# Conditional attention on one NeuronCore: the value products moved behind output blocks in a hand-written order

## The chip, the cores and the metric

The kernel runs on one core of a Trainium2 chip. The metric is the device time of one launch in microseconds. Most executions of one kernel agree within 0.3%.

## The reference, cut to what matters

For each of 16 batches (D = 512 channels, T = 1024 tokens, 8 heads of 64) the reference computes attention in which queries, keys and values are one projection, with a 0/1 mask per token, and adds the result to the input:

```python
q = transpose(x) @ Wq.T                       # T x D
scores = scale * einsum('bhqd,bhkd->bhqk', qh, qh)
logits = (scores * cmask + (1.0 - cmask) * NEG) * rmask
attn = softmax(logits)
out = (attn @ qh) @ Wo.T
y = x + transpose(out)
```

About half of the tokens are active. A masked key gets no weight. A masked query has only zeros for logits, so it averages all values.

## The kernel before, in words

The active tokens of a batch (384 to 544 of 1024) are gathered into C = 544 slots: four blocks of 128 and a tail of 32. Everything below runs over slots. Masked rows get the mean's product, added to their rows and written out as well.

For each batch, in this order of need:

- `xt`: TensorE transposes the gathered rows (L424), and ACT and DVE split them into two float16 parts, `xh` and `xl` (L384, L385).
- `query(n, e, g)`: 12 products with the query weights (L447) for channel block e (0 to 3) and column half g, into a `pm` tile in PSUM. ACT copies it out as q (L450), DVE masks it (L453).
- `qsplit`: DVE makes two float16 parts `hl` of q (L461 to L463), and four DMAs on SP's queue spread them by head into `xx` (L468 to L471). These DMAs are handed to `later`, and are issued at the next step.
- `value(n, e)`: eight short products (L497) of `xx` with a constant turn q's block e into tokens by channels, in a `pm` tile. ACT copies it out as v (L500). Its squares are summed by head into `sd` (L480 on ACT for e = 0, L484 on DVE for the others, L485). `value_tail` does this for the 32 tail tokens (L520).
- the shift, that is the largest squared norm of each head, which keeps the exponential in range, in three parts, for one half g of the heads: `peaks` (DVE, L541 and L543, into `smcol`), `top` (a TensorE transpose, L549, and a DVE maximum `m`, L551), `bottom` (a small product that broadcasts `m`, L558, and DVE and ACT steps from L560 on that make `nm`, the exponential's bias, and `corr`).
- `scores(b, p, i)`: four products per head and row block (L620) into a `pss` tile, of which there are two; ACT takes the exponential and its row sums (L624). The tail's scores are L595 and L599.
- `attend`: p times v, summed in `pav` (L643, the tail L647); ACT copies it out as `c` (L651).
- `recip_sums` and `recip_rows`: the reciprocal row sums, transposed (L680, copied by L683) and sent through DRAM (`rd`, `rb`; L685, L688); `norm` multiplies `c` with `rb` (L711 on) and splits it into `ch` and `cl`.
- `project(o, i)`: 12 products with the output's weights (L727) for row block i; DVE adds them to the gathered rows (L732), and POOL scatters these to the output (L811). `project_tail` does it for the tails of three batches at once, in every third batch.

`pm` has two buffers. All products named except scores and attention take a `pm` tile in turn, so each waits until the one two places earlier has been read out.

The order is written by hand in `run`. One loop runs over batches b. While the scores and attention of b run (18 steps), a list `m` of other work is spread between them: the rest of batch b's own preparation (fourth value, second half of the shift), the output of batch o = b - 1, and the x transposes, queries, values and first half of the shift of batch n = b + 1. Each entry is a cost and a function. `fill` calls entries until their summed cost reaches the step's share, so an entry's place in `m` and the costs ahead of it decide between which scores it stands. Costs in use: value 0.45 (`value` of the own batch) or 0.25, query 1.37, projection 2.6, top and bottom 0.1 each, the others mostly 0. A tile scheduler then arranges the instructions of each engine close to the order of these calls; entries under `high_priority` may come earlier. Each engine takes its instructions in order.

The names in `m`: `sums`, `rows`, `second`, `third` are the reciprocal steps of o's last head pair and the norms of its pairs 2 and 3; `x` the five transposes; `pk`, `tp`, `bt` are peaks, top and bottom; `q` query with qsplit; `v` value; `tc`, `tv` the tail's copy and value; `P_` the output block; `tail` the tail's output; `rng` range checks; `hot`, `index`, `take` prepare and gather batch b + 2; `rest` adds the mean to masked rows.

Of the kernel before, what the change touches and what calls it, by code (L numbers as in the profile page):

```python
# [49 lines left out]
class Fast:  # L50
# [794 lines left out]
    def run(self, flag):  # L845
        B = self.B
        L = lambda f, *a: lambda: f(*a)
# [5 lines left out]
        def xt(n):  # L853
            return [(0.45, L(self.xt, n, c)) for c in range(4)] + [(0.25, L(self.xt, n, 4))]

        def query(n, e, g):
            u = [(1.37, L(self.query, n, e, g))]
            return u + [(0, L(self.qsplit, n, e))] if g else u

        def value(n, e):  # L860
            return [(0.45, L(self.value, n, e))]

        def project(o, *i):
            return [(2.6, L(self.project, o, k)) for k in i]
# [80 lines left out]
        if True:  # L945
            for b in range(B + 1):
                o, n = b - 1, b + 1
# [3 lines left out]
                free, sums, rows, third, tail, rest = {}, [], [], [], [], []  # L951
                if b:
                    sums, rows, third = [(0, L(self.recip_sums, o, 3))], [(0.1, L(self.recip_rows, o, 3))], [(0, L(self.norm, o, 3))]
                if n < B:
                    if b in tails:
                        free[0] = [L(self.late, o, 4)]
                        tail = [(2.6, L(self.project_tail, o))]
# [3 lines left out]
                second = [(0, L(self.norm, o, 2))] if b else []  # L961
                P_ = (lambda *i: project(o, *i)) if b else (lambda *i: [])
                pk, tp, bt = ((lambda o, g, f=f, c=c: [(c, L(f, o, g))]) for f, c in ((self.peaks, 0), (self.top, 0.1), (self.bottom, 0.1)))
                new = [g for g in groups if b == g[0] - 2], [g for g in groups if b == g[0] - 1]
                if n < B:
                    q, x, v = (lambda e, g: query(n, e, g)), xt(n)[2 if b == 0 else 0:], (lambda e: [(0.25, L(self.value, n, e))])
                    tc, tv = ((lambda g, f=f, c=c: [(c, L(f, n, g))]) for f, c in ((self.tail_copy, 0), (self.value_tail, 0.25)))
                    rng = [(0, L(self.range_x, n, c)) for c in range(DC)]
                    ahead = b + 2 < B
                    hot, index = ([(c, L(f, b + 2))] if ahead else [] for f, c in ((self.hot, 0), (self.index, 0.2)))  # L970
                    take = [(0, L(self.gather, b + 2, j)) for j in range(5)] if ahead else []
                    m = sums + x[:2] + (value(b, 3) if b else []) + pk(b, 1) + second + x[2:4] + rows + x[4:]
                    for g in new[0]:
                        m += [(0, L(self.active, *g))]
                    m += q(0, 0) + tp(b, 1) + (q(0, 1) if b else bt(b, 1) + q(0, 1))
                    for g in new[0]:
                        m += [(0.3, L(self.slots, *g))]
                    for g in new[1]:
                        m += [(0, L(self.facts_sums, *g))]
                    m += (bt(b, 1) if b else hot) + q(1, 0) + third + ([] if b else index) + q(1, 1) + ([] if b else take)  # L980
                    for g in new[1]:
                        m += [(0.1, L(self.facts_end, *g))]
                    m += rng[:2] + tc(0) + tail + v(0) + P_(0) + tv(0) + rest + v(1) + P_(1) + (hot if b else []) + rng[2:] + q(2, 0) + (index if b else [])
                    m += pk(n, 0) + q(2, 1) + tp(n, 0) + P_(2) + (take if b else []) + q(3, 0) + v(2) + bt(n, 0)
                    m += q(3, 1) + tc(1) + [(0, L(self.means, n))] + P_(3) + tv(1)
                    if b == 0:
                        k = next(k for k, (c, f) in enumerate(m) if f is index[0][1])
                        for c in range(DC):
                            m.insert(k + 1 + 3 * c, (0, L(self.split, "o", c)))
                else:  # L990

                    places = [("xi", 8), ("xa", 13)]
                    come = [[L(self.late, x, j, *places[k % 2]) for j in range(5, 9)] for k, x in enumerate(rests[b])]
                    leave = [[L(self.rest, x, j) for j in range(5, 9)] for x in rests[b]]
                    free[0] = [L(self.late, b, 4)] + come[0]
                    for c, l in zip(come[1:] + [[]], leave):
                        free[0] += c + l
                    m = second + sums + value(b, 3) + pk(b, 1) + rows + [(0.6, lambda: None)]
                    m += tp(b, 1) + [(0.6, lambda: None)] + bt(b, 1) + [(2.6, L(self.project_means, b))] + third + [(1.2, lambda: None)] + P_(0, 1, 2, 3)
# [4 lines left out]
                if b == 0:  # L1004
                    m = begin + m
# [204 lines left out]
```

## Time and profile before

| what | value |
|---|---|
| median of 3 runs | 1081.12 us (1079.87 to 1084.78) |
| the profiled execution | 1081.4 us |
| its span, first to last instruction | 1079.7 us |
| mean granted TensorE clock | 0.995 |
| busy: TensorE matmul, weight load | 1038.1 us, 690.9 us |
| busy: DVE, ACT, POOL | 745.6 us, 681.6 us, 303.0 us |
| DMA moved | 181.39 MB, mean 168 GB/s |

The profile is that of one execution. The busy time of an engine is the time that its instructions cover; matmuls overlap, and a matmul's own duration is longer than its distance to the next. A row such as `PE pm L497 <- DMA xx<-hl: 11.4, 15, 1.9` says that TensorE sat idle ahead of the instruction at line 497, which writes the tile pm, until the DMA from hl into xx had landed: 11.4 us in total, 15 times, 1.9 us the longest. A timeline row gives start and duration in us, engine, line, operation, output and input, shapes, count, and in brackets the idle time ahead of it. A row of windows gives a stretch of the span, its length, the busy time of each engine with the number of its instructions, the granted clock, the mean busy share of the DMA engines and what they moved in GB/s. Operations recorded as L497 are those that this line of the kernel issues.

### The profile page before, as it was taken

Reading aid. Unit: us, or ns where it says so; the run is one execution under the profiler, and the core shown is the slowest. Engines: PE = TensorE matmul, PEld = TensorE weight load, DVE = VectorE, ACT = ScalarE, POOL = GpSimd, SP = SyncE. Lnnn points to the kernel's source line nnn. Section 1 sums busy time; section 2 is a strip of 40 time slices with the busy share of each in tenths; the row PEclk is TensorE's granted clock in tenths of the full one; section 3 lists DMA queues with packets and bytes.
Section 4 is the critical chain, followed back from the end, with each engine's and each line's share of the span. In section 5 each row is a group of like instructions: output and inputs, shape, how many; then the busy total and the mean of one; then the engine's idle time right before and its main releaser. Section 6 shows DMA issues by size and latency. Waiting matters only on the chain.

```text
span 1079.7 us, 23837 instructions
## 1 busy us (share of the span) xinstructions
PE 1038.1 (96%) x8626; PEld 690.9 (64%) x8626; DVE 745.6 (69%) x2376; ACT 681.6 (63%) x1722; POOL 303.0 (28%) x303
## 2 busy tenths in 40 slices
PE   6889999999999999999999999999999999999996
PEld 6566667666666666666666666667666665666553
DVE  6687768676675767766785776868667775666553
ACT  5777667666676766666576666666666565665550
POOL 3101022222202223222233323222232331335652
PEclk9999999999999999999999999999999999999999
DMA  6746465556655554656556566554755554565752
GB/s 205 211 126 177 133 175 154 174 150 190 174 141 158 171 173 145 198 176 169 177 147 197 154 186 193 152 171 135 229 176 173 177 149 127 149 182 166 222 175 84
DMA packets 78125, 181.39 MB, mean 168 GB/s; under 512 B 15008, under 2 KB 16800, under 8 KB 78000
## 3 DMA queue, kind: packets, MB, share of 16 engines
q1 hardware_dynamic: 56816, 111.62, 36.6%
q0 software_dynamic: 21184, 68.18, 20.8%
q8 instruction: 70, 1.15, 0.5%
q14 instruction: 55, 0.45, 0.1%
HBM read 92.34 MB, written 33.91 MB: 117 GB/s over the span
## 4 chain that ended last, share of the span: by engine, by line
PE 82%; DMA 7%; DVE 3%; ACT 2%; issue 2%; SPq 2%; POOL 0%; POOLq 0%; ACTq 0%; DVEq 0%
PE pav L643 21%; PE pss L620 19%; PE pm L727 15%; PE pm L447 14%; DMA xx<-hl 6%; PE pm L424 3%; PE pav L647 3%; PE pss L595 2%; PE pm L497 2%; PE pm L680 1%; ACT q L450 1%; SPq L470 1%; ACT p L624 1%; PE pm L520 1%; DMA rb<-rd 1%
## 5 line engine op out<-in xcount | busy, mean ns | idle before, releaser
L624 ACT ACTIVATE p<-pss,nm 128x544 f32<-128x544 f32 x512 | 365.5, 717 | 210.5 <-PE pss L620 203.6
L620 PE MATMUL pss<-xx 128*128 128x272 f16 x2048 | 317.6, 280 | 3.1 <-ACT p L624 2.7
L643 PE MATMUL pav<-p,v 128*64 128x272 f32 x2048 | 262.9, 399 | 0.0
L620 PEld LDWEIGHTS <-xx 128*128 128x128 f16 x2048 | 191.9, 100 | 73.2 <-issue 27.7
L643 PEld LDWEIGHTS pav<-p,v 128*64 128x64 f32 x2048 | 135.6, 136 | 94.3 <-issue 27.1
L811 POOL DMA_INDIRECT y_out<-xa,idx x68 | 70.2, 1032 | 288.6 <-issue 91.5
L447 PE MATMUL pm<-xh,wqh 128*128 128x274 f16 (+1 forms) x512 | 143.3, 280 | 3.3 <-DVE nm L560 1.9
L447 PE MATMUL pm<-xl,wqh 128*128 128x274 f16 (+1 forms) x512 | 142.9, 279 | 0.2 <-DVE xl L385 0.2
L447 PE MATMUL pm<-xh,wql 128*128 128x274 f16 (+1 forms) x512 | 143.0, 279 | 0.0
L339 POOL DMA_INDIRECT xa<-x_in,idx x68 | 69.5, 1023 | 167.1 <-PE pss L620 71.0
L447 PEld LDWEIGHTS <-wqh 128*128 128x128 f16 x1024 | 99.3, 98 | 25.9 <-issue 6.7
L811 POOL DMA_INDIRECT y_out<-xi,idx x60 | 74.0, 1233 | 137.7 <-DVE xi L798 38.3
L624 ACT ACTIVATION_READ_ACCUMULATOR p<-pss,nm 128x1 f32 x512 | 102.6, 200 | 0.0
L450 ACT ACTIVATE q<-pm 128x272 f32<-128x272 f32 (+1 forms) x128 | 50.8, 397 | 81.6 <-PE pm L447 81.6
L727 PE MATMUL pm<-woh,ch 128*128 128x512 f16 x240 | 91.8, 382 | 0.3 <-DVE tmp L523 0.3
L727 PE MATMUL pm<-wol,ch 128*128 128x512 f16 x240 | 91.7, 382 | 0.0
L727 PE MATMUL pm<-woh,cl 128*128 128x512 f16 x240 | 91.5, 381 | 0.0
L732 DVE SCALAR_TENSOR_TENSOR xa<-pm,xa 128x512 f32<-128x512 f32 x60 | 41.4, 690 | 72.4 <-PE pm L727 72.3
L339 POOL DMA_INDIRECT xi<-x_in,idx x60 | 61.3, 1021 | 106.1 <-PE pss L620 49.5
L727 PEld LDWEIGHTS <-ch 128*128 128x128 f16 x480 | 46.7, 98 | 45.6 <-issue 2.2
L369 ACT ACTIVATE xm<-xm 128x1024 f32<-128x1024 f32 (+1 forms) x62 | 62.5, 1009 | 2.3 <-DMA xm<-x_nat_in 2.3
L711 DVE TENSOR_TENSOR c<-c,rb 128x544 f32<-128x544 f32 x64 | 46.1, 720 | 22.4 <-PE pss L620 11.1
(194 smaller groups left out, 1550.0 us busy)
## 6 DMA issues: line engine op xcount, KB each, us to landing
xx<-hl SPq DMA_DIRECT2D x256, 136.0 KB
xm<-x_nat_in SPq DMA_DIRECT2D x56, 512.0 KB
rb<-rd SPq DMA_DIRECT2D x128, 136.0 KB
pt<-c SPq DMA_DIRECT2D x64, 136.0 KB
pt<-p SPq DMA_DIRECT2D x64, 136.0 KB
ub<-ud SPq DMA_DIRECT2D x16, 256.0 KB
xi<-x_nat_in SPq DMA_DIRECT2D x8, 256.0 KB
xa<-x_in,idx POOLq DMA_INDIRECT x68, 4.5
```

The source lines that it names most:

```text
L339: dma = self.nc.gpsimd.indirect_dma_start(out=tile[:n], out_offset=None, in_=self.x, in_offset=bass.IndirectOffsetOnAxis(ap=idx, axis=0))
L369: self.nc.scalar.activation(s["xm"][k], s["xm"][k], AF.Copy, accum_out=s["ms2"][:, k:k + 1])
L424: self.pe = nc.tensor.transpose(pt[:, c, :], x[:n, c * P:(c + 1) * P], self.ident[:n, :n]).ins
L447: self.beat = nc.tensor.matmul(pq, lhsT=w[:, c, e * P:(e + 1) * P], rhs=xx[:, c, cols], start=(k == 0), stop=(k == 3 * DC - 1)).ins
L450: nc.scalar.activation(s["q"][:, e, cols], pq, AF.Copy, scale=1.0 / (SX * SW))
L620: self.beat = nc.tensor.matmul(pt[:, g, :CH], lhsT=xx[:, 2 * k, i * P:(i + 1) * P], rhs=xx[:, 2 * k + a, g * CH:(g + 1) * CH], start=(a == ...
L624: self.exp = [nc.scalar.activation(t.rearrange("p (g c) -> p g c", g=2), pt[:, :, :CH], AF.Exp, bias=s["nm"][p // HG][:, p % HG:p % HG + 1 ...
L643: mm = nc.tensor.matmul(s["pav"][k * DK:(k + 1) * DK, g, :CH], lhsT=s["v"][p][:, i, k * DK:(k + 1) * DK], rhs=ps[k][:, cols], start=(i == ...
L711: self.once(nc.vector.tensor_tensor(c, c, s["rb"][p], ALU.mult), self.beat if p < 3 else None)
L727: nc.tensor.matmul(po[:cols.stop - cols.start], lhsT=a[:, e, cols], rhs=w[:, e, :], start=(e == 0 and k == 0), stop=(e == DC - 1 and k == 2))
L732: self.nc.vector.scalar_tensor_tensor(x, po, 1.0 / (SX * SW), x, ALU.mult, ALU.add)
L811: dma = self.nc.gpsimd.indirect_dma_start(out=self.out, out_offset=bass.IndirectOffsetOnAxis(ap=idx, axis=0), in_=x, in_offset=None)
```

## The change

Only the order of entries in `m` changes, at three places. In batch b, the fourth value and the peaks of the second half move from behind the second x transpose to behind the fourth and the fifth; top of the second half moves from ahead of the second query product to behind it. For batch n, the first value goes behind the first output block, the second one behind the second output block and the third query's first half, the third one behind the last query product; the peaks of the first half go behind one more query product, and its top behind the third output block. No instruction is added or taken away, and no cost is changed.

```diff
-                    m = sums + x[:2] + (value(b, 3) if b else []) + pk(b, 1) + second + x[2:4] + rows + x[4:]
+                    m = sums + x[:2] + second + x[2:4] + (value(b, 3) if b else []) + rows + x[4:] + pk(b, 1)
...
-                    m += q(0, 0) + tp(b, 1) + (q(0, 1) if b else bt(b, 1) + q(0, 1))
+                    m += q(0, 0) + (q(0, 1) + tp(b, 1) if b else tp(b, 1) + bt(b, 1) + q(0, 1))
...
-                    m += rng[:2] + tc(0) + tail + v(0) + P_(0) + tv(0) + rest + v(1) + P_(1) + (hot if b else []) + rng[2:] + q(2, 0) + (index if b else [])
-                    m += pk(n, 0) + q(2, 1) + tp(n, 0) + P_(2) + (take if b else []) + q(3, 0) + v(2) + bt(n, 0)
-                    m += q(3, 1) + tc(1) + [(0, L(self.means, n))] + P_(3) + tv(1)
+                    m += rng[:2] + tc(0) + tail + P_(0) + v(0) + tv(0) + rest + P_(1) + (hot if b else []) + rng[2:] + q(2, 0) + v(1) + (index if b else [])
+                    m += q(2, 1) + pk(n, 0) + P_(2) + (take if b else []) + tp(n, 0) + q(3, 0) + bt(n, 0)
+                    m += q(3, 1) + v(2) + tc(1) + [(0, L(self.means, n))] + P_(3) + tv(1)
```

## The prediction

> **What bounds the kernel now.** I read the page's busy times first, then TensorE's groups and waits, then its timeline around one wait, then windows cut from one batch to the next.
>
> ```profile
> PE 1038.1 (96%) x8626; PEld 690.9 (64%) x8626; DVE 745.6 (69%) x2376; ACT 681.6 (63%) x1722; POOL 303.0 (28%) x303
> ```
>
> TensorE (PE) is the only engine that is nearly full. 1079.7 - 1038.1 = 41.6 us of it is idle, so no reordering can win much over 4%, while each new gap in its stream is paid in full. Who ends its gaps (total, times, longest):
>
> ```profile
> PE pm L497 <- DMA xx<-hl: 11.4, 15, 1.9
> ...
> PE pss L620 <- ACT p L624: 2.7, 4, 1.1
> ...
> PE pm L447 <- DVE nm L560: 1.9, 2, 1.4
> PE pm L497 <- ACT qt L508: 1.3, 1, 1.3
> ```
>
> L497 is the value's product, which the change moves. It is the largest waiter, and it waits for the spread copy xx. One such wait in TensorE's timeline (start, duration), and the last issue of that copy on SP's queue:
>
> ```profile
> 438.65 0.19 PE L497 MATMUL pm<-two,xx 128*128 128x64 f16 x1
> 438.68 0.63 PE L620 MATMUL pss<-xx 128*128 128x272 f16 x4
> 439.15 0.38 PE L727 MATMUL pm<-woh,ch 128*128 128x512 f16 x1
> 440.19 0.38 PE L497 MATMUL pm<-two,xx 128*128 128x64 f16 x7 [0.67 <-DMA xx<-hl]
> 440.41 0.38 PE L727 MATMUL pm<-wol,ch 128*128 128x512 f16 x1
> ```
>
> ```profile
> 435.55 0.58 SPq L471 DMA_DIRECT2D xx<-hl  x1
> ```
>
> The value's second product stands in front of the output's products (L727), which need nothing late. TensorE takes its queue in order, so they wait with it. The windows start at each batch's first x transposes; columns: span, busy of PE, PEld, DVE, ACT, POOL, clock, DMA share.
>
> ```profile
> 291.38:353.62 62.24, 62.15 (x525) 41.89 (x524) 41.86 (x130) 41.52 (x105) 9.90 (x10) 1.00 0.51 145
> ...
> 418.71:483.06 64.35, 63.09 (x540) 42.28 (x539) 47.82 (x161) 42.02 (x105) 18.44 (x18) 1.00 0.57 170
> 483.06:547.83 64.77, 62.50 (x526) 41.83 (x524) 44.60 (x138) 41.87 (x105) 17.67 (x17) 1.00 0.61 168
> ...
> 870.53:937.89 67.36, 64.21 (x525) 42.11 (x524) 44.54 (x138) 41.85 (x105) 17.66 (x17) 0.97 0.54 146
> ```
>
> A batch without such a wait takes 62.24 us (the first row; TensorE idle 0.09). The others are longer by what they wait, and the last by more than its waits:
>
> ```profile
> 890.00:894.00 4.00, 1.47 (x15) 0.88 (x16) 2.52 (x10) 1.53 (x5) 0.98 (x1) 1.00 0.99 252
> 893.90:897.40 3.50, 3.50 (x12) 1.23 (x9) 0.69 (x1) 1.22 (x2) 0.00 (x0) 0.52 0.74 166
> ```
>
> The DMA engines are full (0.99) while the copy is awaited, two waits of 1.91 and 1.15 us leave TensorE busy for 1.47 of 4 us, and then its clock is 0.52 for 3.5 us.
>
> **What goes.** Batches with a tail product (from 162, 353, 547, 741 us) already have 12 output products ahead of the first value product, and wait 0.09, 0.09, 0.29 and 0.09 us. That is what the change gives the other batches, so it is the best evidence here. In the seven others that wait, span less PE busy is 0.86 + 1.26 + 2.27 + 1.09 + 1.79 + 1.36 + 3.15 = 11.8 us. From it I take the 1.9 of L447 waiting for nm, which is another chain and stays, and 0.6 that the wait-free batch would idle too (7 x 0.09): 9.3. With two small waits of the third value product (0.20 at 600 us, 0.49 at 991) it is 10.0. Their busy time also falls, since a matmul in front of a wait counts with its whole duration and not with the spacing to the next: 62.50, 62.50, 62.47, 62.36 against 62.15 make 1.2; about 0.3 in each of the two batches with slot products, an estimate from the same rows; and 2.06 in the slow-clock batch, of which 3.4 x 0.5 = 1.7 is the clock. Together 3.9. In the first batches one wait (1.29 at 85.45) gets a query product ahead of it. Sum: 10.0 + 3.9 + 1.3 = 15.2 us.
>
> **Is the new place late enough?** The first value product now follows the first output block (12 x 0.216 = 2.6 us) and scores, attention, a row transpose, scores, tail attention and scores, which took 442.78 to 446.95 = 4.2 us: 6.8 us of cover. The worst batch waited 3.1 us in all. The second moves behind another block, two scores and a query product. The third moves behind the last query product, 1.4 us for waits up to 0.5.
>
> [...]
>
> [...]
>
> **What is added.** No instruction is added. Each value has 8 short products, one ACT copy of 0.59, a square (ACT or DVE, 0.63 to 0.69) and a reduce of 0.68; peaks are two DVE steps of 0.15, top a transpose and a reduce of 0.28, bottom a product, seven small DVE steps and one on ACT. None issues a DMA. Three covers get thinner in the changed order.
>
> (a) Top and bottom of the second half (L549, L558) stood a query product apart. In 7 of 14 batches only four scores (0.47 us) lie between now; in the others attention does (2 us). Today:
>
> ```profile
> 492.51 0.27 PE L549 MATMUL pm<-ident,smcol 128*128 128x128 f32 x1
> ...
> 494.97 0.28 PE L558 MATMUL pm<-ident,m 128*128 128x4 f32 x2
> ```
>
> ```profile
> 491.98 0.15 DVE L543 TENSOR_TENSOR smcol<-smcol,sdt 128x4 f32<-128x4 f32 x1
> ...
> 493.67 0.29 DVE L551 TENSOR_REDUCE m<-pm 128x1 f32<-128x128 f32 x1
> ```
>
> From 492.51 m is ready 1.45 us later when DVE is occupied; at 461.54 it took 0.60. The new distance is 0.11 + 0.47 = 0.6. So a wait is 0 to 0.85. DVE has q's mask (L453) in front of m, which ends 0.95 after the query product, and m 0.29 behind it: about 0.2. Behind a waiting bottom stand the query product and its ACT copy, and nobody else late. 7 x 0.2 = 1.4.
>
> (b) The fourth value of a batch now follows all four x transposes and the tail attention. ACT has an exponential (0.9) and the attention's copy (0.6) ahead of its copy, and the small x transpose needs that PSUM buffer back 1.3 us after the product's start, by today's spacings; today the copy is done 1.03 us after that start and nobody waits. With both ahead of it, it would be done after 2.1: 0 to 0.8 per batch, and 0.1, nearer to today's row, is taken: 14 x 0.1 = 1.4. Later, smcol is ready 0.37 us before top today, with 5.6 us between value and top; now it is 5.4: still about 0.1 spare.
>
> (c) The index product needs the buffer of a query product 1.1 us back, whose ACT copy may stand behind an exponential: 0 to 0.6 in 9 batches, 0.1 taken: 0.9.
>
> Norms stand ahead of more x transposes on DVE; it idled 1.59 us there, which covers a 0.72 us step. On SP, one quarter of a spread now precedes the two row copies rb, which wait over 2 us for their own source anyway; on POOL the scatters keep their number, and TensorE waits for none. Both cost 0; if rb came late, the third norm and with it the output products would wait, up to the 2.3 us that DVE once waited for rb.
>
> Costs 3.7, bounds -3 (fewer splits of products, 31 fewer runs on TensorE, and the nm wait gone) and 12. The profiled execution took 1081.4: 1079.7 and 1.7 around it; the median is 1081.12, 0.3 lower. 1081.4 - 15.2 + 3.7 = 1069.9, say 1070.
>
> **Rivals.** One: the small waits of (a) to (c) take most of it back. The upper ends of half the batches, about 0.8 us each, give 14 x 0.8 = 11: 1077. For it: TensorE is 99.9% busy in a quiet batch, so any lost cover shows. Against: such short covers exist today (0.37 us at top) and cost nothing listed.
>
> Two, slower: the shift's chain becomes the pace. If ACT's copy of the fourth value lands 1 us later, smcol is late by about 0.9 at top, and m at bottom by another 0.85, in 14 batches: 24.5 us against 15.2, so 1081.4 + 9.3 = 1091. It decides from 1.1 us per batch on; over 0.5% slower needs 1.5. For it: both links sit on DVE's in-order queue. Against: DVE idles a third of the time, and a late top also gives m's queue time to drain.
>
> Three: the change does not do what it says, because the waits reappear at the next user of xx, or DMA saturation moves too: 1081. Against: the tail batches have that order and hardly wait.
>
> **How the numbers follow.** The likeliest case has 0.64, rival one 0.20, two 0.13, three 0.03. About 0.5% (5.4 us) is what a measurement of this kernel tells from no change; below 1075.7 lies the likeliest case and a fifth of rival one: faster 0.68, same 0.19, slower 0.13. The range goes from the full gain with all small savings (1081.4 - 15.2 - 3 - 2 = 1061) to 1083, which takes in rivals one and three and leaves out most of two.
>
> **What would show it.** Right: L497's waits for xx under 2 us in TensorE's waits, batches of 62.2 to 62.8 us (65 with a tail), the clock not halved in mid-run. (a) shows as L558 waiting for m, (b) as L424 or L549 waiting for ACT or smcol, (c) as L272 waiting for q. Wrong: batches over 63.5 us without an xx wait, or xx waits at other lines.

## The result and the profile after

| what | before | after |
|---|---|---|
| median of 7 runs | 1080.67 us (1079.87 to 1084.78) | 1073.09 us (1070.37 to 1076.70) |
| ratio after/before, 95% interval | | 0.9927 [0.9906, 0.9948] |
| the profiled execution, its span | 1081.4 us, 1079.7 us | 1075.62 us, 1073.9 us |
| the twelve batches from the fourth marker on | 775.41 us | 768.31 us |

The change makes the kernel faster by 7.6 us, 0.7%. The markers are the first x transposes of a batch, as in the prediction. The twelve batches between the fourth and the sixteenth, the last of them (162.48 to 937.89 us before, 164.42 to 932.73 after) are the steady part, and their sum is used below, because the start differs more from one execution to the next. From the page of after, the busy times of the engines; then windows of before and of after, for the start and the twelve batches:

```profile
PE 1041.8 (97%) x8626; PEld 695.0 (65%) x8626; DVE 744.3 (69%) x2376; ACT 676.7 (63%) x1722; POOL 323.4 (30%) x303
```

```profile
0.00:162.48 162.48, 143.53 (x1280) 101.70 (x1281) 115.96 (x396) 109.33 (x284) 24.80 (x42) 0.99 0.61 171
162.48:937.89 775.41, 762.99 (x6366) 509.55 (x6365) 546.29 (x1733) 503.80 (x1264) 214.51 (x203) 1.00 0.58 169
```

```profile
0.00:164.42 164.42, 146.12 (x1281) 104.63 (x1281) 115.40 (x396) 109.74 (x284) 28.12 (x42) 0.96 0.61 170
164.42:932.73 768.31, 764.11 (x6365) 510.81 (x6364) 545.08 (x1733) 499.49 (x1264) 233.84 (x203) 1.00 0.59 170
```

The span is 5.8 us shorter, but TensorE is busy for 3.7 us more (1038.1 before). Of these, 2.6 lie in the start, where this execution had more half clock (granted clock 0.96 against 0.99; in the first 50 us it was 0.97 in before and in e1, 0.90 in e10 and 0.86 in after). The other 1.1 lie in the twelve batches, which are 7.1 us shorter: their idle time fell from 12.4 to 4.2 us, and their busy time rose, where the prediction had it fall by 3.9. So something was given back there that this view counts as work. The end, from the last marker on, changed by 0.6 us.

TensorE's waits after (total, times, longest):

```profile
PE pss L620 <- ACT p L624: 2.0, 3, 1.0
PE pm L447 <- DVE xa L732: 1.8, 5, 0.4
...
PE pm L497 <- DMA xx<-hl: 0.6, 1, 0.6
```

In the whole run the value product waits for the spread copy once, 0.6 us, where it waited 11.4 us in 15 places. The waits for nm are gone too; in the batch from 677 us a query product waits 0.45 us for another step of DVE (L202) instead. Of the rows that before does not have, one comes in five batches: query products (L447) wait for L732, the addition of an output block. The windows, one batch each:

```profile
293.73:356.58 62.85, 62.60 (x524) 42.04 (x523) 41.87 (x130) 41.45 (x105) 12.55 (x10) 1.00 0.51 143
356.58:422.55 65.97, 65.49 (x537) 43.27 (x535) 45.51 (x142) 41.74 (x106) 18.06 (x17) 1.00 0.59 176
...
485.67:548.53 62.86, 62.61 (x525) 42.06 (x524) 44.47 (x138) 41.53 (x105) 20.41 (x17) 1.00 0.64 175
...
869.88:932.73 62.85, 62.60 (x524) 42.04 (x523) 44.80 (x138) 41.45 (x105) 20.39 (x17) 1.00 0.57 155
sum 768.31, PE 764.11 PEld 510.81 DVE 545.08 ACT 499.49 POOL 233.84; mean PE 63.68 PEld 42.57 DVE 45.42 ACT 41.62 POOL 19.49
```

The sum is that of all twelve rows. The batch from 485 us, which took 64.77, and the one from 870, which took 67.36, are down to 62.86 and 62.85. But the quiet batch, for which no wait was listed and which took 62.24, now also takes 62.85 (0.61 more), and a batch with a tail 65.97 instead of 65.09 (0.88 more). That is the part given back.

### Where the quiet batch's 0.61 us sits

No row of waits names it: of the 0.61 us, 0.45 is counted as busy. It shows in the distances between groups, from the start of one product to the start of the next. First, top and bottom of the second half, TensorE and then DVE of after:

```profile
305.32 0.27 PE L549 MATMUL pm<-ident,smcol 128*128 128x128 f32 x1
305.43 0.63 PE L620 MATMUL pss<-xx 128*128 128x272 f16 x4
306.16 0.36 PE L558 MATMUL pm<-ident,m 128*128 128x4 f32 x2
```

```profile
305.49 0.33 DVE L453 TENSOR_TENSOR q<-q,hr 128x160 f32<-128x160 f32 x1
305.73 0.28 DVE L551 TENSOR_REDUCE m<-pm 128x1 f32<-128x128 f32 x1
```

The four scores end their turn at 305.43 + 0.47 = 305.90 by the usual distance; bottom starts at 306.16. In between it waits for m, which DVE began behind q's mask and finished at 306.01. That is 0.26 us, and it comes so in seven batches.

Second, the index product (L272) of a batch without a tail, which now stands behind the second value and four scores. TensorE, then ACT, of after:

```profile
458.93 0.34 PE L272 MATMUL pm<-oht,tmp 128*128 128x9 f16 x8
```

```profile
456.75 0.71 ACT L624 ACTIVATE p<-pss,nm 128x544 f32<-128x544 f32 x1
457.36 0.19 ACT L624 ACTIVATION_READ_ACCUMULATOR p<-pss,nm 128x1 f32 x1
457.45 1.04 ACT L369 ACTIVATE xm<-xm 128x1024 f32<-128x1024 f32 x1
...
458.49 0.38 ACT L450 ACTIVATE q<-pm 128x272 f32<-128x272 f32 x1
```

The index product takes the pm buffer of the query product two places earlier, and needs ACT's copy of it (L450) to be done. That copy stands behind an exponential and behind a range step (L369) of 1.04 us, ends at 458.87, and the product starts at 458.93. Its distance to the scores ahead is 0.75 us instead of 0.46: 0.29 us. So it is in all nine batches without a tail that have an index product. In the eight of them among the twelve, scores that follow a query product 33 us into the batch also start 0.25 us behind it, where 0.12 is usual: 0.13 more.

Against these stands a delay that before had and after has not, and that no row of waits names. In each of the twelve batches of before, the query product that follows top of the second half starts 0.25 us late. TensorE of before:

```profile
300.94 0.40 PE L620 MATMUL pss<-xx 128*128 128x272 f16 x2
301.42 0.28 PE L447 MATMUL pm<-xh,wqh 128*128 128x274 f16 x1
```

Two scores take 0.23 us by the usual distance, so the query could start at 301.17. It takes the pm buffer of the query product ahead of top, and the profile names ACT's copy of that (L450) as what released it. With top behind both query products this delay is gone. Together 0.26 + 0.29 + 0.13 - 0.25 and 0.06 for the fourth value's place (e9 and e10 below) make 0.49 of the 0.61 us; the rest lies in smaller distances that are not traced here.

The tail batches have in addition the listed wait. TensorE at the query product behind top, and DVE's addition that it waits for:

```profile
216.23 0.28 PE L447 MATMUL pm<-xh,wqh 128*128 128x272 f16 x1 [0.37 <-DVE xa L732]
```

```profile
215.50 0.68 DVE L732 SCALAR_TENSOR_TENSOR xa<-pm,xa 128x512 f32<-128x512 f32 x1
```

Top's transpose used to stand ahead of the output block; now it is the only pm tile between that block's last product and the query, so the query's tile is the block's own, and DVE reads it out until 216.18. By its distance the query is 0.53 us late; 0.37 of that is counted as idle.

The tail batches lose 0.28 us more near their end, which no row lists, at scores that stand among the products of the fourth output block. TensorE, then ACT, of after:

```profile
415.53 0.39 PE L727 MATMUL pm<-woh,ch 128*128 128x512 f16 x1
416.02 0.62 PE L620 MATMUL pss<-xx 128*128 128x272 f16 x4
```

```profile
414.35 0.58 ACT L500 COPY v<-pm 128x512 f32<-128x512 f32 x1
...
415.17 0.71 ACT L624 ACTIVATE p<-pss,nm 128x544 f32<-128x544 f32 x1
415.77 0.19 ACT L624 ACTIVATION_READ_ACCUMULATOR p<-pss,nm 128x1 f32 x1
```

The scores usually follow an output product by 0.22 us; here it is 0.49. They need a pss tile back from the exponential, which is done at 415.96, and the third value's copy (L500) stands ahead of that on ACT. The delay is in all four tail batches of after, e2, e5, e6 and e7, and in none of the other kernels: those five have the third value and the first half's peaks in their new places. Which of the two moves it is was not tried.

### The profile page after: what moved, and what is told of

Same layout as the page of the kernel before. It is cut to its first block, busy times and chain, and to the rows that moved or that the text cites. A ratio compares the mean times of both kernels' runs of the same rounds, so it can differ in the third digit from the quotient of the medians.

```text
span 1073.9 us, 23845 instructions
## 1 busy us (share of the span) xinstructions
PE 1041.8 (97%) x8626; PEld 695.0 (65%) x8626; DVE 744.3 (69%) x2376; ACT 676.7 (63%) x1722; POOL 323.4 (30%) x303
## 3 DMA queue, kind: packets, MB, share of 16 engines
q0 software_dynamic: 21184, 68.18, 20.9%
q8 instruction: 70, 1.15, 0.5%
## 4 chain that ended last, share of the span: by engine, by line
PE 85%; ACT 6%; DVE 3%; DMA 3%; issue 2%; SPq 0%; POOL 0%; POOLq 0%; DVEq 0%; ACTq 0%
PE pav L643 23%; PE pss L620 19%; PE pm L447 15%; PE pm L727 15%; PE pm L424 3%; ACT p L624 3%; PE pav L647 3%; PE pss L595 2%; PE pm L497 1%; PE pm L680 1%; ACT xm L369 1%; DMA xx<-hl 1%; PE pm L520 1%; PE pm L558 1%; DMA pt<-p 1%
## 5 line engine op out<-in xcount | busy, mean ns | idle before, releaser
L447 PE MATMUL pm<-xh,wqh 128*128 128x274 f16 (+1 forms) x512 | 143.7, 281 | 2.4 <-DVE xa L732 1.8
L447 PE MATMUL pm<-xh,wql 128*128 128x274 f16 (+1 forms) x512 | 143.1, 279 | 0.0
L447 PE MATMUL pm<-xl,wqh 128*128 128x274 f16 (+1 forms) x512 | 143.0, 279 | 0.0
L339 POOL DMA_INDIRECT xa<-x_in,idx x68 | 94.9, 1395 | 151.2 <-PE pss L620 50.4
L447 PEld LDWEIGHTS <-wqh 128*128 128x128 f16 x1024 | 98.0, 99 | 26.3 <-issue 7.7
L450 ACT ACTIVATE q<-pm 128x272 f32<-128x272 f32 (+1 forms) x128 | 50.8, 397 | 84.9 <-PE pm L447 84.6
L811 POOL DMA_INDIRECT y_out<-xi,idx x60 | 70.8, 1180 | 104.9 <-PE pss L620 46.0
L732 DVE SCALAR_TENSOR_TENSOR xa<-pm,xa 128x512 f32<-128x512 f32 x60 | 41.4, 690 | 71.6 <-PE pm L727 71.5
L369 ACT ACTIVATE xm<-xm 128x1024 f32<-128x1024 f32 (+1 forms) x62 | 62.4, 1006 | 2.0 <-DMA xm<-x_nat_in 2.0
```

The lines of the kernel that those rows point to most:

```text
L339: dma = self.nc.gpsimd.indirect_dma_start(out=tile[:n], out_offset=None, in_=self.x, in_offset=bass.IndirectOffsetOnAxis(ap=idx, axis=0))
L369: self.nc.scalar.activation(s["xm"][k], s["xm"][k], AF.Copy, accum_out=s["ms2"][:, k:k + 1])
L447: self.beat = nc.tensor.matmul(pq, lhsT=w[:, c, e * P:(e + 1) * P], rhs=xx[:, c, cols], start=(k == 0), stop=(k == 3 * DC - 1)).ins
L450: nc.scalar.activation(s["q"][:, e, cols], pq, AF.Copy, scale=1.0 / (SX * SW))
L732: self.nc.vector.scalar_tensor_tensor(x, po, 1.0 / (SX * SW), x, ALU.mult, ALU.add)
L811: dma = self.nc.gpsimd.indirect_dma_start(out=self.out, out_offset=bass.IndirectOffsetOnAxis(ap=idx, axis=0), in_=x, in_offset=None)
```

## The experiments

In the table, "quiet" is the batch that begins near 290 us, "tail" the one after it; "nm batch" begins near 675 us and held the wait for nm; "twelve" is the sum of the twelve batches. Ratios are against runs of the kernel before in the same session: its medians there were 1080.86 (e1 to e4), 1080.52 (e5 to e8) and 1087.82 (e9 to e11, on record as the same chip as e1 to e4). For the last session the ratio and the batches are compared, and not the us; times 1080.7 a ratio is brought to the scale of the others. A batch's length is from one execution: e1 and its repeat e11 differ by 0.95 us in the twelve.

| kernel | median us | ratio, 95% interval | quiet | tail | nm batch | twelve |
|---|---|---|---|---|---|---|
| before | 1080.67 | 1 | 62.24 | 65.09 | 64.85 | 775.41 |
| after | 1073.09 | 0.9927 [0.9906, 0.9948] | 62.85 | 65.97 | 63.70 | 768.31 |
| e1, first value alone | 1068.07 | 0.9881 [0.9860, 0.9902] | 62.28 | 65.07 | 64.48 | 762.30 |
| e2, next batch's part alone | 1073.40 | 0.9937 [0.9921, 0.9954] | 62.64 | 65.85 | 64.75 | 767.92 |
| e3, own batch's part alone | 1077.02 | 0.9955 [0.9938, 0.9972] | 62.39 | 65.12 | 64.56 | 771.16 |
| e4, less traffic | 1060.71, one run | | 62.22 | 65.10 | 62.84 | 760.68 |
| e5, after, second value back | 1066.28 | 0.9864 [0.9838, 0.9890] | 62.46 | 65.80 | 62.71 | 763.92 |
| e6, after, top back | 1071.54 | 0.9915 [0.9886, 0.9944] | 62.84 | 65.59 | 63.56 | 766.53 |
| e7, after, bottom apart | 1069.28 | 0.9895 [0.9866, 0.9924] | 62.53 | 65.91 | 63.62 | 765.99 |
| e8, e1 with the own batch's part | 1065.68 | 0.9848 [0.9818, 0.9877] | 62.42 | 65.11 | 62.75 | 761.00 |
| e9, e8 with bottom apart | 1069.99 | 0.9836 [0.9814, 0.9859] | 62.08 | 65.60 | 63.30 | 760.37 |
| e10, e9 with the fourth value as before | 1069.44 | 0.9836 [0.9812, 0.9860] | 62.02 | 65.00 | 63.50 | 760.06 |
| e11, e1 again | 1073.71 | 0.9875 [0.9853, 0.9897] | 62.27 | 65.08 | 64.48 | 763.25 |

### e1: the first value alone

The kernel before, with one entry moved:

```diff
-                    m += rng[:2] + tc(0) + tail + v(0) + P_(0) + tv(0) + rest + v(1) + P_(1) + ...
+                    m += rng[:2] + tc(0) + tail + P_(0) + v(0) + tv(0) + rest + v(1) + P_(1) + ...
```

> Only the first value of the next batch goes behind the first output block; all else is as before. Theory (this one place is the whole gain, the other moves only cost): TensorE's waits for xx at L497 fall from 11.4 to under 2 us, ordinary batches take 62.2 to 62.4 us, median 1066 to 1069. Rival (the whole set is needed, because the second value, which now stands close behind, waits in its place): xx waits of 4 us or more and 1073 or above.

TensorE's waits in e1, and windows of it: the twelve batches, then a quiet batch, the nm batch, and the last of the twelve:

```profile
PE pm L497 <- DMA xx<-hl: 3.3, 5, 1.4
...
PE pm L447 <- DVE nm L560: 1.5, 1, 1.5
```

```profile
161.88:924.18 762.30, 759.49 (x6366) 510.10 (x6365) 543.24 (x1733) 501.57 (x1264) 216.47 (x203) 1.00 0.60 172
```

```profile
289.89:352.17 62.28, 62.19 (x525) 41.92 (x524) 41.29 (x130) 41.41 (x105) 9.73 (x10) 1.00 0.53 144
669.77:734.25 64.48, 62.92 (x541) 42.37 (x540) 47.54 (x159) 41.86 (x105) 18.18 (x17) 1.00 0.58 167
861.90:924.18 62.28, 62.19 (x525) 41.90 (x524) 44.10 (x138) 41.41 (x105) 17.70 (x17) 1.00 0.58 158
```

One moved entry brings 12.8 us, more than the whole change. The twelve batches lose 13.1 us: 9.6 of idle time (12.4 to 762.30 - 759.49 = 2.8) and 3.5 of busy time (762.99 to 759.49). The quiet batch keeps its 62.28, and the clock in the last batch stays at 1.00. The wait for nm stays. The waits for xx are 3.3 us in all, where under 2 was expected, but none of them lies in the twelve batches. So the mechanism of the gain is the one predicted, and the rest of the change costs 5.0 us by the medians (6.0 in the twelve batches).

### e2 and e3: the two parts of the change, each alone

e2 has only the third place of the diff (batch n, the last three lines), e3 only the first two places (batch b's fourth value, peaks and top):

```diff
# e3
+                    m = sums + x[:2] + second + x[2:4] + (value(b, 3) if b else []) + rows + x[4:] + pk(b, 1)
...
+                    m += q(0, 0) + (q(0, 1) + tp(b, 1) if b else tp(b, 1) + bt(b, 1) + q(0, 1))
```

> The third part of the change alone (values 0, 1, 2 and first-half shift of the next batch); the own batch's fourth value and second-half shift stay as before. Theory: no xx waits, and the lost cover at the index product (L272, 0.3 us in 9 batches) as the main cost: ordinary batches 62.4 to 62.6 us, 1069 to 1071. Rival (all the cost of the change lies in this part): ordinary batches 62.85 as in the changed kernel, 1073.

> The first two parts of the change alone (fourth value behind the x transposes, peaks, top and bottom of the second half later). Theory: the xx waits of the first value stay, and 0.3 us at the fourth value and 0.27 us between top and bottom come on top: 1082 to 1087. Rival (fewer splits of products pay for it, or this part gains by itself): 1080 or less.

A quiet batch of e2, then of e3 together with the batch from 870 us, and e3's waits:

```profile
289.66:352.30 62.64, 62.48 (x525) 41.95 (x524) 41.70 (x130) 41.48 (x105) 12.53 (x10) 1.00 0.52 143
```

```profile
292.57:354.96 62.39, 62.28 (x525) 41.99 (x524) 41.73 (x130) 41.27 (x105) 9.73 (x10) 1.00 0.52 145
870.85:934.87 64.02, 62.58 (x524) 41.86 (x523) 44.54 (x138) 41.36 (x105) 17.48 (x17) 1.00 0.55 153
```

```profile
PE pm L497 <- DMA xx<-hl: 12.8, 13, 1.8
```

e2 missed what I expected: 1073.4 where I had 1069 to 1071, and its quiet batch lies 0.04 us above the range; the median is the rival's, the batch is not (62.64, not 62.85). Of the quiet batch's 0.6 us, the next batch's part brings 0.40 and the own batch's part 0.2 (62.64 to 62.85; alone, 0.15). e3 missed too, with the other sign: I expected the own batch's part to cost, and alone it makes the kernel faster by 0.45%, though the waits for xx are all there (12.8 us). Three things pay for it. The waits for nm are gone (the nm batch is still long, for two waits for xx; the other batch that had one, from 418.71 us in before, takes 62.77 instead of 64.35). The 0.25 us delay behind top is gone from every batch, so that the own order costs 0.15 us a batch and not 0.4. And the batch from 870 us takes 64.02 instead of 67.36: its wait of 1.32 us came once, not as a pair, and no half clock followed. Whether the moved entries made a single wait of the pair, or the one execution looked at did, stays open.

### e4: the same order with less traffic

```diff
# the gathers, additions and scatters of masked rows inside the loop are left out
-                    for x in rests.get(b, []):
+                    for x in []:
```

> The kernel before, without the gathers, additions and scatters of the masked rows of the batches that are handled inside the loop (their outputs are left out; those of the last batch stay). TensorE's order is unchanged. Theory (the copy xx is late because other transfers fill the DMA engines): the xx waits at L497 fall from 11.4 to under 4 us. Rival (the copy is late because DVE and SP's queue issue it late): 8 us or more stay.

TensorE's waits for xx in e4, and one ordinary batch; then the last issue of the spread copy for the first value in a batch of before (from 806.81 us) and in the same batch of e4 (from 856.44):

```profile
PE pm L497 <- DMA xx<-hl: 1.2, 3, 0.6
```

```profile
476.45:538.88 62.43, 62.32 (x525) 41.98 (x524) 41.77 (x134) 41.49 (x105) 8.67 (x9) 1.00 0.49 142
```

```profile
822.31 0.65 SPq L471 DMA_DIRECT2D xx<-hl  x1
```

```profile
871.91 0.60 SPq L471 DMA_DIRECT2D xx<-hl  x1
```

TensorE's instructions stand in the old order, with the value products in their early place, and yet the wait falls from 11.4 to 1.2 us. DVE and POOL have less to do in e4 as well, but the copy is not issued earlier for it: 15.50 us into the batch in before, where the value then waits 1.27 us, and 15.47 in e4, where it waits for nothing. In another batch (from 613.29 us in before, wait 0.93) e4 issues it 0.56 us later and does not wait either. So the copy is late because other transfers are under way, as the prediction read from the DMA share of 0.99; the early place alone is not the cause. The time is one run of a kernel that does less, and is no version to use.

### e5, e6 and e7: the change with one entry put back

```diff
# e5: the second value back ahead of its output block
-                    ... + rest + P_(1) + (hot if b else []) + rng[2:] + q(2, 0) + v(1) + (index if b else [])
+                    ... + rest + v(1) + P_(1) + (hot if b else []) + rng[2:] + q(2, 0) + (index if b else [])
# e6: top of the first half back ahead of the third output block
-                    m += q(2, 1) + pk(n, 0) + P_(2) + (take if b else []) + tp(n, 0) + q(3, 0) + bt(n, 0)
+                    m += q(2, 1) + pk(n, 0) + tp(n, 0) + P_(2) + (take if b else []) + q(3, 0) + bt(n, 0)
# e7: bottom of the second half behind the next query product
-                    m += (bt(b, 1) if b else hot) + q(1, 0) + third + ...
+                    m += ([] if b else hot) + q(1, 0) + (bt(b, 1) if b else []) + third + ...
```

> The changed kernel with the second value put back ahead of the second output block. Theory (the index product loses its cover because the second value stands between it and the third query's first half, 0.29 us in each of 9 batches): the gap of 0.75 us from the scores to the index product closes to 0.47, ordinary batches 62.45 to 62.6 us instead of 62.85, median 1070 to 1071. Rival (the cost lies with the other moves): ordinary batches 62.8, 1073.

> The changed kernel with the top of the next batch's first half put back ahead of the third output block. Theory (in the five tail batches the query product behind top needs the buffer of the third output block, which DVE at L732 has not read out): the 0.36 us waits of L447 for L732 go, tail batches 65.4 to 65.6 us instead of 65.97, ordinary batches stay at 62.85, median 1070.5 to 1072. Rival (that wait only gives way to another one): tail batches stay at 65.9, 1073.

> The changed kernel with the bottom of the second half put behind one more query product, so that top and bottom stand apart again. Theory (bottom waits 0.27 us for m in 7 batches): the four scores between top and bottom take 0.47 us again instead of 0.73, and ordinary batches 62.6 instead of 62.85; median 1071 to 1072. Rival (the time at bottom was not a wait for m): 62.85 and 1073.

A quiet batch of e5 and the index product in it; a tail batch of e6; a quiet batch of e7:

```profile
289.40:351.86 62.46, 62.34 (x525) 41.90 (x524) 41.70 (x130) 41.45 (x105) 12.55 (x10) 1.00 0.53 145
```

```profile
324.17 0.62 PE L620 MATMUL pss<-xx 128*128 128x272 f16 x4
324.63 0.35 PE L272 MATMUL pm<-oht,tmp 128*128 128x9 f16 x8
```

```profile
545.20:610.80 65.60, 65.48 (x536) 43.44 (x535) 45.59 (x142) 41.87 (x106) 19.02 (x18) 1.00 0.61 181
```

```profile
292.00:354.53 62.53, 62.38 (x524) 42.08 (x523) 41.86 (x130) 41.45 (x105) 12.53 (x10) 1.00 0.51 145
```

Each of the three places is confirmed by what its undoing gives back. With the second value in its old place, the index product is again 0.46 us behind its scores, and the 0.13 us at the scores ahead goes too; the quiet batch gains 0.39 us, and the waits for xx do not return for it (2.0 us in the whole of e5). e5 came out below its expectation (1066.28 for 1070 to 1071), since more hung on the second value than the index product. With top back, the waits for L732 vanish and a tail batch takes 65.60 instead of 65.97: its busy time is the same, 65.48, and only the idle 0.4 us goes. With bottom behind the query product, the quiet batch gains 0.32 us (the median, 1069.28, was expected at 1071 to 1072). In the twelve batches this is 4.4, 1.8 and 2.3 us. The intervals of the ratios of e6 and of e7 overlap that of after; these two stand on the lengths of their batches, not on the median.

### e8 to e11: putting the better parts together

e8 is e1 with the two lines of e3. e9 is e8 with bottom of the second half behind the query product as in e7. e10 is e9 with the fourth value where the kernel before has it:

```diff
# e10 against e9
-                    m = sums + x[:2] + second + x[2:4] + (value(b, 3) if b else []) + rows + x[4:] + pk(b, 1)
+                    m = sums + x[:2] + (value(b, 3) if b else []) + second + x[2:4] + rows + x[4:] + pk(b, 1)
```

> The first value of the next batch behind the first output block, and the first two parts of the change. Theory (the own batch's part gained 0.45% alone only by moving the xx waits and one wait for nm; its own order costs 0.1 to 0.15 us per ordinary batch): with the xx waits gone nothing is left to gain, ordinary batches 62.4, median 1067 to 1070, no better than the first value alone at 1068. Rival (the two gains add): 1063 to 1065.

> The kernel before, with the first value behind the first output block, the own batch's fourth value, peaks and top of the second half in their later places, and bottom of the second half behind one query product, so that it no longer follows top within four scores. Theory: the costs add up from short distances, and the wait at bottom is one of them that can be removed alone: batches without a tail 62.1 to 62.2 us (62.4 with bottom in its old place), the batch that waits for nm near 62.5 and not 64.5, total 1062 to 1064. Rival: bottom's place only moves the wait to the next product in the rotation of the two pm buffers: batches stay at 62.4, total 1065 to 1067.

> As the previous kernel of this call, but the fourth value stays where the kernel before has it; only the peaks, top and bottom of the second half go later. It tells which part of the own batch's move takes away the wait for nm (1.5 us, once, in the kernel with the first value moved alone) and which part costs the 0.15 us of a quiet batch. Theory: the fourth value's place costs the 0.15 us and is not needed against the nm wait, since that is the second half's chain: quiet batches 62.2, no nm wait, total 1062 to 1064, level with or below the previous kernel. Rival: the nm wait needs the fourth value out of the way of the exponentials on ACT: one batch of 64.4 us again, total 1066 to 1068.

> The kernel before with the first value alone behind the first output block, a second time, now on the same chip as the two others of this call, so that what the own batch's part adds to it is read from one comparison. Theory: 1067 to 1069 as in the first comparison, 4 to 5 us above the two others. Rival: the difference of 2.4 us to the kernel with the own batch's part was the chips' or the half-clock spells' at the start: all three within 1.5 us of each other.

The nm batch of e8; then a quiet and the nm batch of e10, and the nm batch of e11:

```profile
670.06:732.81 62.75, 62.74 (x540) 42.54 (x539) 47.51 (x159) 41.53 (x105) 18.32 (x17) 1.00 0.60 171
```

```profile
292.24:354.26 62.02, 62.02 (x524) 41.88 (x523) 41.55 (x130) 41.55 (x105) 9.87 (x10) 1.00 0.51 146
672.00:735.50 63.50, 62.87 (x541) 42.27 (x540) 47.65 (x159) 41.62 (x105) 18.39 (x17) 1.00 0.59 169
```

```profile
673.35:737.83 64.48, 62.92 (x540) 42.35 (x539) 47.39 (x159) 41.93 (x105) 18.09 (x17) 1.00 0.59 167
```

e8 came between the two expectations, and what it has over e1 is in the nm batch: 62.75 instead of 64.48. In the last session e9 and e10 both reach 0.9836, which is 1063.0 us on the scale of the others, and e1's repeat 0.9875, or 1067.2. The difference of 4 us within one comparison (1069.44 and 1069.99 against 1073.71) agrees with the 3 us of the twelve batches (760 against 763.25): the gains add, though the intervals of e9 and of e10 both touch that of e11. TensorE in e10's quiet batch is busy for all of its 62.02 us; that batch is shorter than before's 62.24, since the 0.25 us delay behind top is gone and neither bottom nor the index product waits. e10 also has no nm wait, so the fourth value need not move against that wait: peaks, top and bottom do it. Its nm batch still waits 0.63 us for another step of DVE (L196), and takes 63.50 where e8's takes 62.75; that of e9 missed the 62.5 expected in the same way (63.30). The fourth value's later place costs 0.06 us a batch (62.08 to 62.02); in two of e9's four tail batches (65.60, the others 65.45 and 65.07) a query product waits 0.56 and 0.55 us for ACT, which e10 does not have. Both versions beat the kernel before and, by ratios whose intervals do not touch, the changed one; e8, e9 and e10 can't be told apart by their intervals.

## Why the prediction was right, point by point

- **The direction and the mechanism.** Right. The waits for xx end because the first value got output products ahead of it (e1), and they existed because of traffic (e4). 1073.1 lies 3 us above the predicted 1070.0, within the range.
- **The gain, 10.0 idle and 3.9 busy.** Right in size and in its two parts: e1 shows 9.6 and 3.5 in the twelve batches. What the prediction got wrong is which entry earns it. The waits for xx in the seven batches all stand at the first value; the second had none, and its move brought nothing that shows and cost 4.4 us in the twelve batches. The third had two small ones (0.20 and 0.49); the first of them is gone in e1 without its move, and the third's move alone was not tried.
- **The nm wait.** The prediction left its 1.9 us in place as another chain. It is gone in after and e3 and stays in e1 and e2, so the own batch's part removes it, and e10 narrows that to peaks, top and bottom of the second half. About 1.5 us of gain was thus missing from the sum, of which after gives back 0.45 in the wait for L202.
- **The half clock, 1.7 us.** There is none in mid-run in after nor in e1, as predicted: the granted clock is 1.00 in each of the twelve batches of after and in the last of e1's, where the last of before has 0.97. In e1, from 890 to 894 us, the place of the pair of waits before:

```profile
890.00:894.00 4.00, 4.00 (x35) 2.24 (x32) 3.15 (x7) 3.10 (x9) 0.92 (x1) 1.00 0.28 100
```

  Behind the first 50 us and ahead of the end it was seen twice. In before it came directly behind the two waits of 1.91 and 1.15 us. In e7 it came behind a single one, at 85 us; a row of its timeline, then a window:

```profile
86.49 0.20 PE L497 MATMUL pm<-two,xx 128*128 128x64 f16 x1 [1.85 <-DMA xx<-hl]
```

```profile
87.42:90.83 3.41, 3.41 (x22) 2.43 (x21) 1.71 (x4) 1.91 (x5) 0.00 (x0) 0.50 1.04 257
```

  Single waits of 1.67 and 1.79 us in e3 had none behind them, nor had the two of 1.38 and 1.68 us in after near 90 us (granted clock 1.00 from 85 to 100 us). That the waits caused it, as the prediction assumed when it counted the 1.7 us as gone, fits both times, and is not shown: TensorE was busy for 1.47 of the 4 us ahead of it in before, and for 1.54 of the 3.4 us ahead of it in e7.
- **The start, 1.3 us.** Not seen. The wait at 85 us went, but two others appeared there (L497 for cth 1.4, L647 for pt 1.7). The fourth marker comes 1.9 us later than before; how much of that is the half clock at the start (0.86 against 0.97 in the first 50 us) can't be read from one execution.
- **Cost (a), bottom waits for m.** Right in place, mechanism (m behind q's mask on DVE) and nearly in size: 0.26 us against 0.2 a batch. It came in the seven batches named, and e7 gives back 2.3 us for the twelve. What the prediction did not see at this place is a gain: top's old place delayed the next query product by 0.25 us in every batch, 3.0 in the twelve, and that is gone.
- **Cost (b), the fourth value.** Right in size: 0.1 us a batch predicted, 0.06 between e9 and e10. Where in the batch it sits is not shown, so its mechanism is open.
- **Cost (c), the index product.** The place was right, the size was not: 0.29 us at the product in the nine batches named, 0.39 per quiet batch in e5 with the scores ahead of it, against 0.1. The bounds were 0 to 0.6, worked out with an exponential on ACT; the instruction that decided was the range step L369 of 1.04 us right behind it, which stands there in all nine. This is the term that was mis-sized most.
- **What was not in the sum.** The query product behind top in the five tail batches waits 0.36 us for L732 and is 0.53 late by its distance. The prediction looked at what moved products need, and not at who takes their pm buffer two places later. e6 gives back 0.38 us per tail batch. The 0.28 us at the scores behind the third value's copy was not in it either.
- **The sum of costs.** 3.7 predicted. After lies 6.0 us above e1 in the twelve batches although it has no nm wait (1.5), so the net cost is 7.5 us, twice the estimate and inside the bounds of -3 to 12. In these batches the undoing gives back 4.4 (e5, in which the wait for L202 goes as well), 1.8 (e6) and 2.3 (e7); with 12 x 0.06 for the fourth value and 4 x 0.28 at the scores the new delays come to 10.3 us. The delay of 12 x 0.25 that is gone takes 3.0 off, which leaves 7.3 of the 7.5, within the 1 us by which two executions of one kernel differ. So the new delays were put at about a third of what they are, and a gain that the prediction did not have made up for part of it; that the time came within 3 us of the forecast owes something to luck.
- **The late copy.** In the rows of the prediction the product that waits for the copy starts at 440.19, 4.6 us after the copy's last issue at 435.55. e1 and e4 show that the wait was real.
- **The rivals.** Rival one (small waits take most of it back, 1077) named the right kind of cost and overstated it; the result lies between it and the likeliest case. Rival two, the chain as the pace, did not come: the delay at bottom ended at 0.26 us, far from the 1.1 us a batch from which it would decide. Rival three did not come either: no other user of xx waits in the twelve batches.
- **The marks.** Waits for xx under 2 us: 0.6. Batches of 62.2 to 62.8, 65 with a tail: 62.85 and 65.97, just above, by (c) and the L732 wait. One sign of being wrong came in one batch, the nm batch: 63.70 without a wait for xx. It is one of the two with slot products, and it has the wait for L202. The marks named for (a) to (c), rows of waits at L558, L549 and L272, were not the way to see them: they showed as distances.

## What to carry to other kernels

When one instruction at the head of a full engine's queue waits for a transfer, move that one, and only as far as its worst wait asks: the first value alone earned 13.1 us, and its companions, which had next to no waits of their own (0.7 us in two places), took back half of it. For each product that is moved through a rotation of two buffers, look up whose buffer it takes and who takes its own two places later, and what stands on ACT and DVE ahead of that read-out, long steps that seem unrelated among them. Look also for such a delay in the old order, which a move can end: top's old place cost 0.25 us a batch and stood in no row of waits. On an engine that is 99% busy compare the periods of equal batches and the distances between groups: 0.45 us of the 0.61 that a quiet batch lost was counted as busy.

## What the runs showed of the hardware that was not expected

Gaps of 0.15 to 0.3 us ahead of a product hardly become idle time in the record, because the recorded duration of the matmuls ahead is longer than their distance to the next (0.63 us against 0.47 for four scores) and covers most of them: with the same products in the same clock, the twelve batches of after have 4.6 us more busy time than those of e1 (764.11 and 759.49). The late spread copy is a matter of load: in e4 the indirect transfers move 42.61 MB instead of 68.18, the mean DMA share falls from 0.58 to 0.52, and the waits for xx from 11.4 to 1.2 us. In e7 a half clock of 3.4 us (granted clock 0.50) followed a single wait of 1.85 us, with TensorE busy for 1.54 of the 3.4 us ahead of it. And two sessions on what is on record as one chip ran the kernel before 0.64% apart (1087.82 and 1080.86); of the 6.0 us by which the profiled executions of e1 and its repeat differ, 0.95 is in the twelve batches (763.25 and 762.30), and the rest is in the start and the end. What makes the sessions differ is open.
